# First expert layer: a table of tokens by lane and tile, and rows gathered from a copy in DRAM, in place of per-expert row lists

## The chip, the core and the metric

The kernel runs on one core of a Trainium2 chip. TensorE (PE in the profile) multiplies matrices, VectorE (DVE) and ScalarE (ACT) work on elements, GpSimd (POOL) issues the indirect DMAs and does small elementwise work, and SyncE (SP) issues most of the other DMAs. [...] The metric is the device time of one execution in microseconds (us), as the median of several runs.

## The reference

Four layers follow one another on a batch of 8 x 512 tokens of 256 numbers, each with a residual and a layer norm: a recurrent block of three layers; an expert layer with 8 experts; an attention of 16 heads; a second expert layer with 16 experts, 4 for each token. The change concerns the first expert layer:

```python
logits = xt @ Wg                                   # xt: 4096 x 256
probs = softmax(logits);  pT = probs.T
_, top_idx = top_k(pT, cap)                        # cap = 4096 / 8: each expert picks its tokens
sel = zeros((E, T), bool).at[arange(E)[:, None], top_idx].set(True)
tok2exp = where(sel.any(axis=0), argmax(where(sel, pT, -inf), axis=0), argmax(pT, axis=0))
weights = take_along_axis(probs, tok2exp[:, None], axis=1)[:, 0]
out = sum over e of where(tok2exp == e, weights, 0)[:, None] * (gelu(xt @ W1[e]) @ W2[e])
```

So in the end each token belongs to one expert, and has one weight. The next thing that happens to the result is the layer norm of `x + out`, at the head of the attention layer.

## The kernel before, in words

`x_tok` holds all tokens in SBUF: 128 partitions by 32 chunks (`NC`) of 256 numbers; it is the front part of `x_ext`, whose rows have 276 numbers (`RW`), with room for a gate weight and two row numbers. The stages are these.

1. **Recurrent block** (`recurrent_layers`), 12 pairs of stages. Its SP queue also zeroes the sums of the second expert layer (`acc`) and, at L229, the whole list area `m0rows` in DRAM (8 lists of 4224 rows).
2. **Gates** (`expert_choice_gates`): softmax and a threshold search on DVE and PE; it gives `M`, a one-hot matrix of token and expert, and the weight of each token, written into `x_ext`.
3. **Lists** (`expert_choice_layer` from L1195, class `Lists`). Two products, with ones (`tot`) and with a triangle (`rk`), give each token its place in its expert's list. POOL writes the rows into the lists, one indirect DMA for each of the 32 chunks (`put`, L737); SP closes each list with empty rows (`end_list`, L771). DVE makes two tables: one over the lists' state after half the chunks, from which 8 full tiles (`NE0`) may start early, and one over the rest (`table`, L793 to L826). `fence` (L755) makes POOL wait until the first 16 puts have landed, and then POOL gathers the 8 early tiles (`gather`, L907), with the other puts in between.
4. **Expert tiles** (`Lists.run`): 36 tiles (`ME0`; three more stand in a block that runs only if there are more) of 128 rows of one expert. `turn` transposes the rows (L968, copied at L970), `first` multiplies by W1 and applies gelu (L981, L989), `second` multiplies by W2 (L1003), and `done` adds weight times result to the row (L1261) and scatters the rows to `res` in DRAM (L1264, POOL). The order on PE is first(t), turn(t+1), second(t-1). After second(t-1), tile t+3 is loaded on SP (L960), and its 1 MB of weights if they differ from those of the last tile in the same of four buffers (`NW`; L950, L952). A part of n tiles is dealt out so that each buffer works through n/4 neighbouring entries of the table; the parts are tiles 0 to 7 and 8 to 35. In this stage the order on POOL and SP is the program's.
5. **Rows back** (`rows_back`, L1286): SP loads `res` into `x_tok`, 8 loads of 512 KB, each partition 4 rows of 1 KB that lie one after another. A list row carries the number of the row of `res` that this needs (`place`), so that the tokens come back in another order of the chunks.
6. **Attention** (`attention_layer`), in the program's order on PE, ACT and DVE: layer norm and transposes of each group of four chunks, products for q, k and v, and heads spread over partitions by 8 small DMAs on SP for each half of q or k (`spread_heads`, L1688); the first scores (L1801) need the first half of q's and k's heads. The second expert layer's constants (L728 to L733, L1329 to L1334) are loaded on SP between the rows and the heads.
7. **Second expert layer** (`token_choice_layer`), and the final sums, layer norm and store (L2006 to L2016).

Outside the stages named, a scheduler orders the instructions by program order and readiness.

Of the kernel before, what the change touches and what calls it, by code (L numbers as in the profile page):

```python
# [10 lines left out]
F32 = mybir.dt.float32  # L11
# [6 lines left out]
P = 128  # L18
# [28 lines left out]
NE0 = (NC // 2 * P - E0 * (P - 1)) // P  # L47
# [109 lines left out]
def recurrent_layers(tc, x_tok, xT, lg, ident, eps6, eps5, acc, rows0, a):  # L157
# [11 lines left out]
    with ExitStack() as ctx:  # L169
# [45 lines left out]
        NZ = 1060  # L215
        zero = wp.tile([P, NZ], F32, name="zero1")
        nc.vector.memset(zero, 0.0)
        for x in acc:
            nc.sync.dma_start(
                x[:T, :].rearrange("(p c) d -> p c d", p=P),  # L220
                zero[:, :D].unsqueeze(1).to_broadcast([P, NC, D]),
            )
            nc.sync.dma_start(x[T : T + P, :], zero[:, :D])
# [368 lines left out]
        def late(t):  # L592
# [20 lines left out]
            if N:  # L613
                last_norm(t - 2, 0, NCH)
            inputs(t)
# [22 lines left out]
        def end(u):  # L638
# [20 lines left out]
            last_apply(u - 1, 0, NCH)  # L659
            residual(u, 0)  # L660
# [12 lines left out]
            last_apply(*parts[0])  # L673
            last_apply(*parts[1], on_dve=True)
            for b in (1, 0):
                for i in range(2 * b, 2 * b + 2):
                    last_turn(u, i, on_dve=b == 1)
# [11 lines left out]
class Lists:  # L689
# [6 lines left out]
    def __init__(self, tc, ctx, name, E, NT, a, rows=None):  # L696
# [6 lines left out]
        self.rows = rows  # L703
        if rows is None:
            self.rows = self.dram.tile([E * LT + P, RW], F32, name=f"{name}rows")
# [4 lines left out]
        self.held, self.got = [], {}  # L710
# [171 lines left out]
    def everywhere(self, psum, tag, ident):  # L882


        nc, rp, n = self.nc, self.rp, self.early
        first, spread = rp.tile([P, 1], F32, name="first"), rp.tile([P, n], F32, name="spread")
        nc.vector.tensor_copy(first, self.tabs[0][1][:, 0:1])
        nc.vector.tensor_scalar_mul(spread, ident[:, :n], first)
        self.at_ps = psum.tile([P, n], F32, tag=tag, name="at_ps")
        nc.tensor.matmul(self.at_ps, self.ones, spread, start=True, stop=True)  # L890

    def take_rows(self):
        self.at = self.rp.tile([P, self.early], I32, name="at")
        self.nc.vector.tensor_scalar_add(self.at, self.at_ps, self.pno)

# [7 lines left out]
    def gather(self, t):  # L903

        i = self.entry(t)
        self.got[t] = self.rp.tile([P, RW], F32, name=f"{self.name}got{t}")
        self.reads(self.nc.gpsimd.indirect_dma_start(  # L907
            out=self.got[t], out_offset=None, in_=self.rows[:, :],
            in_offset=bass.IndirectOffsetOnAxis(ap=self.at[:, i : i + 1], axis=0),
            bounds_check=self.E * LT + P - 1, oob_is_err=False,  # L910
        ).ins)
# [11 lines left out]
    def run(self, ctx, ident, w_pack, bias, done, taken=None, besides=None):  # L923
# [16 lines left out]
        xgs, hTs, read = {}, {}, {}  # L940
# [4 lines left out]
        def weights(t):  # L945
            if t < len(self.held):
                return
            w, differs = read.pop(t, None) or known(t)
# [5 lines left out]
        def load(t):  # L954
            if t in self.got:
                xgs[t] = self.got.pop(t)
                return
            xgs[t] = hp.tile([P, RW], F32, tag="xg", bufs=NW + 1, name=f"{nm}xg_{t}")
            at = value(t, 0, E * LT)
            ins = nc.sync.dma_start(xgs[t], self.rows[bass.ds(at, P), :]).ins  # L960
            if t < self.early:
                self.reads(ins)
# [86 lines left out]
        rest(t1)  # L1049

# [125 lines left out]
def expert_choice_layer(tc, pre, x_ext, lg, ident, rows, res, load, a):  # L1176

    nc = tc.nc
    x_tok = x_ext[:, :, :D]
    with ExitStack() as ctx:  # L1180
        L = Lists(tc, ctx, "m0", E0, NT0, a, rows)
        L.constants(a)
# [3 lines left out]
        keep = rp.tile([P, E0, NC], F32, name="keep0")  # L1186
        nc.vector.memset(keep, 1.0)
        nc.vector.memset(keep[:, :, 0:1], 0.0)
        expert_choice_gates(
            nc, rp, psX, ident, lg, a, M, x_ext[:, :, D].rearrange("p (s j) -> p j s", j=2)  # L1190
        )
        load()
# [5 lines left out]
        cnt = rp.tile([P, E0, NC], F32, name="cnt0")  # L1198
        by_expert = tot.rearrange("p c e -> p e c")
        nc.vector.tensor_copy(cnt, by_expert)  # L1200
        nc.vector.tensor_add(cnt[:, :, 0], cnt[:, :, 0], L.off)
        upto = rp.tile([P, E0, NC], F32, name="upto0")
        nc.vector.tensor_tensor_scan(
            upto.rearrange("p e c -> p (e c)"), keep.rearrange("p e c -> p (e c)"),
            cnt.rearrange("p e c -> p (e c)"), 0.0, ALU.mult, ALU.add,
        )
        nc.vector.tensor_sub(cnt, upto, by_expert)
        pl = rp.tile([P, NC, E0], F32, name="pl0")
        slot = rp.tile([P, NC], I32, name="slot0")
        fs = rp.tile([P, NC], F32, name="fs0")  # L1210

        with tc.manual_schedule(engines={mybir.EngineType.DVE, mybir.EngineType.Pool}):
            for i in range(2):
                k = slice(i * NC // 2, (i + 1) * NC // 2)
                nc.vector.tensor_add(pl[:, k], rk[:, k], cnt.rearrange("p e c -> p c e")[:, k])
                nc.vector.tensor_mul(pl[:, k], pl[:, k], M[:, k])
                nc.vector.reduce_sum(fs[:, k], pl[:, k], AX.X)
                nc.vector.tensor_copy(slot[:, k], fs[:, k])
            n, half = (rp.tile([P, E0], F32, name=k) for k in ("n0", "half0"))
            nc.vector.tensor_sub(half, upto[:, :, NC // 2 - 1], L.off)  # L1220
            nc.vector.tensor_sub(n, upto[:, :, NC - 1], L.off)
            L.early, L.breaks = NE0, [ME0]
            L.done = rp.tile([P, E0], F32, name="done0")
            for _, part in L.table(half, 0, 0) + [L.early_tiles()]:
                part()
            L.everywhere(psX, "x", ident)
            for _, part in L.table(n, P - 1, NE0, L.done):
                part()
# [907 lines left out]
```

## Time and profile before

| What | Value |
|---|---|
| Three runs | 1902.87, 1903.4 (median), 1906.02 us |
| Profiled execution, its own time | 1902.39 us |
| Span of its profile | 1900.6 us |
| Granted TensorE clock, mean | 0.946 of full |
| PE, DVE, ACT, POOL busy | 88%, 59%, 52%, 27% of the span |
| Recurrent block ends, gates begin | about 399 us |
| Gates end, lists begin (`tot`) | 453.4 us |
| First transpose of a tile; end of the last product | 488.1; 631.2 us |
| First load of rows back; first scores of the attention | 635.3; 661.6 us |
| Scatters of the second expert layer | 1332 to 1850 us |

The profile is one execution. Times are from the start of its span, which lies 1.8 us inside the execution's own time. PEld is the loading of weights into TensorE, which overlaps the products. A busy time of an engine says little by itself; what counts is which engine the others wait for in each stage. Queues of DMA instructions are SPq, ACTq, POOLq: the time there is that of issuing, not of moving.

### The profile page before, as it was taken

What the parts mean: (1) busy time and instruction counts of PE and PEld (TensorE: products, weight loads), DVE (VectorE), ACT (ScalarE), POOL (GpSimd) and SP (SyncE); (2) the same over time, 40 slices, a digit from 0 to 9 for tenths busy, and PEclk for the clock granted to TensorE, in tenths of its full rate; (3) what the DMA queues carried; (4) which work ended last, traced back from release to release, by engine and by line L of the source; (5) the groups of instructions that cost most, each with busy time, mean ns of one, the idle gap of its engine ahead of it and who ended that gap; (6) DMA issues with size and microseconds to landing.
All of it is one profiled execution on the core that took longest, in us unless ns stands there. A gap on an engine that the chain in (4) does not pass through costs nothing. (4 is left out here: it accounts for less than half of the span.)

```text
span 1900.6 us, 30538 instructions
## 1 busy us (share of the span) xinstructions
PE 1663.6 (88%) x10108; PEld 1086.5 (57%) x10108; DVE 1120.4 (59%) x2827; ACT 992.8 (52%) x2134; POOL 513.2 (27%) x497
## 2 busy tenths in 40 slices
PE   6999997432699799999989999987999999999996
PEld 2555553321699576222222222223889999999985
DVE  6999999775122463777868787884434222222226
ACT  4899986420122342566666766655534333343333
POOL 1000000012622220010221422332666644444440
PEclk9999998765799899999999999998999999999998
DMA  9991000012663400000110111132675658666548
GB/s 357 402 405 42 1 1 0 0 58 101 216 229 122 121 9 6 16 14 18 38 39 18 62 49 30 44 102 75 162 208 129 154 131 230 143 140 140 99 83 266
DMA packets 113249, 211.88 MB, mean 111 GB/s; under 512 B 16749, under 2 KB 84415, under 8 KB 106816
## 3 DMA queue, kind: packets, MB, share of 16 engines
q1 hardware_dynamic: 80672, 161.44, 25.6%
q0 software_dynamic: 29408, 45.80, 11.8%
q10 hardware_dynamic: 3008, 2.63, 0.4%
q8 instruction: 84, 1.38, 0.3%
q14 instruction: 77, 0.63, 0.1%
HBM read 233.05 MB, written 99.12 MB: 175 GB/s over the span
## 5 line engine op out<-in xcount | busy, mean ns | idle before, releaser
L1894 DVE TENSOR_REDUCE nmx<-s 128x1 f32<-128x512 f32 x512 | 329.5, 685 | 125.6 <-PE t L1813 112.4
L1901 ACT ACTIVATE pe<-t 128x512 f32<-128x512 f32 x512 | 277.7, 594 | 184.4 <-PE t L1813 181.4
L1801 PE MATMUL s<-kT,qT 32*128 32x512 f32 x1024 | 289.7, 640 | 46.8 <-ACT pe L1901 27.0
L1813 PE MATMUL t<-qA,kT 32*128 32x512 f32 x1024 | 289.7, 642 | 2.5 <-ACT pe L1901 2.0
L1990 POOL DMA_INDIRECT acc<-y,at x136 | 211.8, 1557 | 244.5 <-DVE at L1983 160.0
L1801 PEld LDWEIGHTS s<-kT,qT 32*128 32x128 f32 x1024 | 78.5, 183 | 195.5 <-ACT pe L1901 182.5
L987 ACT ACTIVATE m1hT<-m1h,m1ws 128x128 f32<-128x128 f32 x272 | 99.4, 367 | 150.5 <-PE m1h L981 135.6
L987 ACT ACTIVATE m1hT<-m1h,xT 128x128 f32<-128x128 f32 x272 | 99.5, 367 | 141.5 <-PE m1h L981 124.5
L1989 DVE TENSOR_SCALAR y<-m1o,gt 128x256 f32<-128x256 f32 x136 | 65.7, 483 | 162.8 <-PE m1o L1003 162.5
L970 DVE COPY m1xq<-m1xp 128x256 f32<-128x256 f32 x136 | 57.6, 423 | 170.7 <-PE m1xp L968 170.5
L737 POOL DMA_INDIRECT m1rows<-x_ext,slot x128 | 127.4, 995 | 113.4 <-ACT pe L1901 73.4
L981 PE MATMUL m1h<-m1xq,xT 128*128 128x128 f32 x1088 | 137.4, 281 | 4.8 <-issue 3.1
L981 PEld LDWEIGHTS m1h<-m1xq,xT 128*128 128x128 f32 x1088 | 135.7, 197 | 8.9 <-issue 3.5
L1837 PE MATMUL po<-pe,V 128*17 128x512 f32 x1024 | 135.6, 602 | 1.2 <-ACT pe L1901 1.2
L981 PEld LDWEIGHTS m1h<-m1xq,m1ws 128*128 128x128 f32 x1088 | 132.7, 193 | 6.9 <-issue 3.6
L981 PE MATMUL m1h<-m1xq,m1ws 128*128 128x128 f32 x1088 | 134.1, 277 | 2.4 <-DVE m1xq L970 2.4
L1003 PE MATMUL m1o<-xT,m1hT 128*128 128x256 f32 x544 | 129.8, 380 | 0.7 <-DVE y L1989 0.5
L1003 PE MATMUL m1o<-m1ws,m1hT 128*128 128x256 f32 x544 | 129.5, 380 | 0.0
L1867 POOL TENSOR_TENSOR AO<-AO,on 128x256 f32<-128x256 f32 x32 | 23.5, 734 | 365.9 <-DVE on L1862 252.3
L1648 POOL MEMSET qT<- 128x512 f32 x2 | 1.0, 524 | 382.2 <-PE lt L522 382.2
L1003 PEld LDWEIGHTS m1o<-xT,m1hT 128*128 128x128 f32 x544 | 97.7, 190 | 11.4 <-issue 1.1
L1003 PEld LDWEIGHTS m1o<-m1ws,m1hT 128*128 128x128 f32 x544 | 98.2, 191 | 10.4
(372 smaller groups left out, 2974.4 us busy)
## 6 DMA issues: line engine op xcount, KB each, us to landing
xT<-in_w_pack SPq DMA_DIRECT2D x68, 1034.0 KB
m1ws<-in_w_pack SPq DMA_DIRECT2D x68, 1034.0 KB
m0ws<-in_w_pack SPq DMA_DIRECT2D x36, 1034.0 KB
m0rows<-zero SPq DMA_DIRECT2D x5, 6360.0 KB
m1xg<-m1rows SPq DMA_DIRECT2D x136, 138.0 KB
acc<-zero SPq DMA_DIRECT2D x2, 4096.0 KB
f<-acc SPq DMA_DIRECT2D x16, 512.0 KB
m0rows<-zero SPq DMA_DIRECT2D x1, 4770.0 KB
```

The lines of the kernel that those rows point to most:

```text
L737: ins = self.nc.gpsimd.indirect_dma_start(out=self.rows[:, :], out_offset=bass.IndirectOffsetOnAxis(ap=place, axis=0), in_=row, in_offset= ...
L970: nc.vector.tensor_copy(xq, ps)
L981: nc.tensor.matmul(ps, w[:, o : o + P], xq[:, dc, :], start=(dc == 0), stop=(dc == DC - 1),)
L987: ins = nc.scalar.activation(hT[:, fc, :], ps, AF.Gelu, bias=w[:, o : o + 1])
L1003: nc.tensor.matmul(ps, hT[:, fc, :], w[:, o : o + D], start=(fc == 0), stop=(fc == FC - 1))
L1801: mm = nc.tensor.matmul(ps, qTs[u % NR][r, qc * P : (qc + 1) * P], kTs[u % NR][r, :], start=True, stop=True,)
L1813: mm = nc.tensor.matmul(ps, kTs[v % NR][r, kc * P : (kc + 1) * P], qAs[v][r, :], start=True, stop=True,)
L1837: mm = nc.tensor.matmul(po[h4 * HP : h4 * HP + VW, :], V[:, b * NQ + kc, 4 * g + h4, :], pes.pop((u, kc, h4)), start=(kc == 0), stop=(kc = ...
L1894: ins = nc.vector.tensor_reduce(at, ps, AX.X, ALU.max, negate=True)
L1901: ins = nc.scalar.activation(pe, ps, AF.Exp)
L1989: nc.vector.tensor_scalar_mul(y, ps, gt)
L1990: nc.gpsimd.indirect_dma_start(out=R.acc[t % 2][:, :], out_offset=bass.IndirectOffsetOnAxis(ap=at, axis=0), in_=y, in_offset=None, compute ...
```

## The change

The lists go. A new class `Gathered` takes the place of `Lists` in the first expert layer (the second keeps `Lists`).

- The recurrent block doesn't zero a list area. When a group of chunks has its last layer norm, SP copies it to `kept` in DRAM (4096 rows of 1 KB, in token order).
- `places` computes for every token its slot in a table of all tiles, each expert's tokens starting on a tile of their own, and splits it into a lane (0 to 127) and a tile. It makes one table of the tiles' experts.
- `invert` turns this round on PE: the sum over the 32 chunks of a one-hot matrix of lanes (128 x 128, made on DVE eight chunks at a time) times a one-hot matrix of 40 tiles that carries the token's number and its weight. The result says for each lane and tile which token stands there (`src`, `dst`) and with which weight (`share`).
- A tile's rows come by an indirect DMA on POOL from `kept` (`fetch`), in the loop and before the loop alike; before, the 28 later tiles came from the lists on SP. The first 36 tiles are one part. Weights are still asked for on SP, the first four after each tile's gather in the program.
- `done` takes weight and destination from the tables; `res` is in token order, so `rows_back` has 32 loads of 128 KB, four for each group, with 32 partitions of four rows of 1 KB each. The third and fourth load of the first group are issued by ACT.

```diff
 def recurrent_layers(...)
-        NZ = 1060
-        zero = wp.tile([P, NZ], F32, name="zero1")
+        zero = wp.tile([P, D], F32, name="zero1")
...
-        n = rows0.shape[0] // P * RW // NZ
-        lists = rows0.rearrange("(p c) w -> p (c w)", p=P).rearrange("p (c z) -> p c z", z=NZ)
-        for c in range(0, n, 12):
-            k = min(n, c + 12) - c
-            nc.sync.dma_start(lists[:, c : c + k], zero.unsqueeze(1).to_broadcast([P, k, NZ]))
...
+        def keep(u, c0, n):
+            l, q = stages[u]
+            at = slice(q * NCH + c0, q * NCH + c0 + n)
+            nc.sync.dma_start(
+                kept.rearrange("(c p) d -> p c d", p=P)[:, at, :], x_tok[:, at, :]
+            )
...
 class Lists:
-    def gather(self, t):
...
+    def fetch(self, t, dst):
+        at = self.value(t, 0, self.E * LT)
+        ins = self.nc.sync.dma_start(dst, self.rows[bass.ds(at, P), :]).ins
...
         def load(t):
-            if t in self.got:
-                xgs[t] = self.got.pop(t)
-                return
...
+            xgs[t] = hp.tile([P, self.width], F32, tag="xg", bufs=NW + 1, name=f"{nm}xg_{t}")
+            self.fetch(t, xgs[t])
...
-        for t in range(0 if bias else NW):
-            weights(t)
-        if besides:
-            besides(-1, None)
-        read.update({t: known(t) for t in range(NW, 0 if bias else self.early)})
         for t in range(NW):
             load(t)
-            if bias:
-                weights(t)
+            weights(t)
...
+class Gathered(Lists):
+    def places(self, M, tot, rk):
+        cnt, upto = (new(k, [P, E, NC]) for k in ("cnt0", "upto0"))
+        by_expert = tot.rearrange("p c e -> p e c")
+        nc.vector.tensor_copy(cnt, by_expert)
+        nc.vector.tensor_tensor_scan(flat(upto), flat(self.keep), flat(cnt), 0.0, ALU.mult, ALU.add)
...
+        nc.vector.tensor_scalar_add(nb_i, upto[:, :, NC - 1], float(P - 1))
+        nc.vector.tensor_single_scalar(nb_i, nb_i, 7, ALU.logical_shift_right)
+        nc.vector.tensor_scalar_mul(nb, nb_i, float(P))
+        nc.vector.tensor_tensor_scan(cum, self.ones[:, :E], nb, 0.0, ALU.mult, ALU.add)
+        nc.vector.tensor_sub(off, cum, nb)
+        nc.vector.tensor_sub(cnt, upto, cnt)
+        nc.vector.tensor_add(cnt, cnt, off.unsqueeze(2).to_broadcast([P, E, NC]))
...
+        nc.vector.tensor_add(pl, rk, cnt.rearrange("p e c -> p c e"))
+        nc.vector.tensor_mul(pl, pl, M)
...
+        nc.vector.reduce_sum(fs, pl, AX.X)
+        nc.vector.tensor_copy(slot, fs)
+        nc.vector.tensor_single_scalar(split[:, 0], slot, P - 1, ALU.bitwise_and)
+        nc.vector.tensor_single_scalar(split[:, 1], slot, 7, ALU.logical_shift_right)
...
+        nc.vector.tensor_copy(self.split, split)
...
+    def invert(self, psum, tag, W):
+        nc, rp, N = self.nc, self.rp, NT0 + 1
...
+        eq, of = new("eq0", [P, NC, N]), new("of0", [P, NC, 2, N])
+        nc.vector.tensor_tensor(eq, row(NC, N), by(self.split[:, 1], NC, N), ALU.is_equal)
+        nc.vector.tensor_mul(of[:, :, 0], eq, by(self.ids, NC, N))
+        nc.vector.tensor_mul(of[:, :, 1], eq, by(W, NC, N))
+        ps = psum.tile([P, 2, N], F32, tag=tag, name="inverse")
+        K = 8
+        for c0 in range(0, NC, K):
+            at = rp.tile([P, K, P], F32, tag="lane", bufs=3, name=f"lane_{c0}")
+            nc.vector.tensor_tensor(
+                at, row(K, P), by(self.split[:, 0, c0 : c0 + K], K, P), ALU.is_equal
+            )
+            for c in range(c0, c0 + K):
+                nc.tensor.matmul(
+                    ps, at[:, c - c0], of[:, c], start=(c == 0), stop=(c == NC - 1)
+                )
...
+        nc.vector.tensor_scalar(self.src, ps[:, 0], -1.0, 0.0, ALU.add, ALU.max)
...
+    def fetch(self, t, dst):
+        i = self.entry(t)
+        self.nc.gpsimd.indirect_dma_start(
+            out=dst, out_offset=None, in_=self.rows[:, :],
+            in_offset=bass.IndirectOffsetOnAxis(ap=self.src[:, i : i + 1], axis=0),
+            bounds_check=T - 1, oob_is_err=False,
+        )
...
 def expert_choice_layer(...)
+        L = Gathered(tc, ctx, "m0", E0, NT0, kept)
+        L.breaks = [ME0]
...
+        with tc.manual_schedule(engines={mybir.EngineType.DVE}):
+            L.places(M, tot, rk)
+            L.invert(psX, "x", W)
...
     def rows_back():
         for g in range(NC // 4):
-            ins = nc.sync.dma_start(
-                x_tok[:, g * 4 : (g + 1) * 4, :], src[:, g * 4 : (g + 1) * 4, :]
-            ).ins
...
+            src = res[g * S : (g + 1) * S, :].rearrange("(i q e) d -> e i q d", q=4, e=4)
+            for e in range(4):
+                queue = nc.scalar if g == 0 and e > 1 else nc.sync
+                ins = queue.dma_start(
+                    x_tok[e * 32 : (e + 1) * 32, g * 4 : (g + 1) * 4, :], src[e]
+                ).ins
```

More of the change, by code (lines that the diff above doesn't have):

```diff
@@ L1207, in expert_choice_layer @@
[L1207 to L1228, printed above, removed]
-            L.ends(n)
-            L.take_rows()
-            L.count_tiles()
-            left = NC
-            def put(k):
-                nonlocal left
-                for c in range(NC - left, NC - left + k):
-                    L.put(slot[:, c : c + 1], x_ext[:, c, :])
-                left -= k
-            put(NC // 2 + 3)
-            L.grown = L.fence(NC // 2)
-            for t in range(NE0):
-                L.gather(t)
-                if t >= NW - 1:
-                    put(min(left, 2))
-            put(left)
@@ L1261, in done @@
             nc.vector.scalar_tensor_tensor(
-                z, ps, row[:, D : D + 1], row[:, :D], ALU.mult, ALU.add
+                z, ps, L.share[:, i : i + 1], row, ALU.mult, ALU.add
             )
@@ L1279, in expert_choice_layer @@
         with tc.manual_schedule(engines={mybir.EngineType.Pool, mybir.EngineType.SP}):
[L1280 to L1281 removed]
+            L.run(ctx, ident, a["w0_pack"], False, done)
     def rows_back():
         for g in range(NC // 4):
[L1286 to L1290 removed]
+            src = res[g * S : (g + 1) * S, :].rearrange("(i q e) d -> e i q d", q=4, e=4)
[4 more added lines that the diff above has]
+                ).ins
+                for last in moved[ME0 - 2 : ME0] + moved[-2:]:
+                    tc.add_manual_dep(ins, last.name, SYNC, reason="all rows are there")
     return rows_back
@@ L2049, in block @@
             weights, load = attention_weights(tc, ep, a)
-            back = expert_choice_layer(tc, pre, x_ext, lg, ident, rows0, res0, load, a)
+            back = expert_choice_layer(tc, pre, x_tok, lg, ident, kept, res0, load, a)
         if stages > 2:
```

151 lines of the change are left out of this document (78 added, 73 removed).

## The prediction, made before the change was run

> **What bounds the kernel now.** I read the page's forty slices first: PE is at 9 or more in most of them and lowest in the eighth to eleventh (4, 3, 2, 6), the end of the recurrent block, the gates and the routing of the first expert layer. The change rewrites the routing and the tiles behind it, so I read those by stage (columns: window; sum; busy time and instructions of PE, PEld, DVE, ACT, POOL; clock; DMA share; GB/s).
>
> ```profile
> 453.00:463.00 10.00, 2.31 (x6) 1.44 (x6) 7.73 (x38) 0.00 (x0) 4.00 (x4) 0.50 0.12 43
> 463.00:473.00 10.00, 0.33 (x2) 0.23 (x2) 2.76 (x23) 1.28 (x1) 7.56 (x9) 0.50 0.94 343
> 473.00:483.00 10.00, 0.00 (x0) 0.00 (x0) 0.00 (x0) 0.00 (x0) 7.08 (x8) 0.50 1.05 380
> 483.00:488.00 5.00, 0.00 (x0) 0.00 (x0) 0.00 (x0) 0.00 (x0) 2.38 (x4) 0.50 0.34 110
> 488.00:498.00 10.00, 9.24 (x46) 8.69 (x47) 1.27 (x3) 2.22 (x8) 7.86 (x8) 0.63 0.34 113
> 560.00:630.00 70.00, 70.00 (x491) 66.16 (x490) 16.82 (x37) 21.07 (x76) 18.46 (x19) 1.00 0.35 112
> ```
>
> From 463 to 488 only POOL works: it writes token rows into the lists. From 488 the tiles keep PE full, to the last product at 631.2. Everything after needs all rows, so a microsecond won before 631 moves the end by one, unless the return of the rows takes it back. The timeline gives the two prices I need most: how a gather becomes a tile, and what a steady tile does.
>
> ```profile
> 484.23 0.10 POOL L755 MEMSET m0full<- 128x1 f32 x1 [2.02 <-DMA m0rows<-x_ext,slot]
> 485.11 1.05 POOL L907 DMA_INDIRECT m0got<-m0rows,at  x1 [0.78 <-POOL m0full L755]
> 488.09 0.66 PE L968 MATMUL m0xp<-ident,m0got 128*128 128x128 f32 x2 [24.77 <-DMA m0got<-m0rows,at]
> ...
> 597.70 1.95 PE L981 MATMUL m0h<-m0xq,m0ws 128*128 128x128 f32 x16
> 597.90 0.48 DVE L1261 SCALAR_TENSOR_TENSOR z<-m0o,m0xg 128x256 f32<-128x256 f32 x1 [1.31 <-PE m0o L1003]
> 598.66 0.97 POOL L1264 DMA_INDIRECT res<-z,m0xg  x1 [2.76 <-DVE z L1261]
> 601.43 1.95 PE L981 MATMUL m0h<-m0xq,m0ws 128*128 128x128 f32 x16
> ```
>
> A gather costs POOL 1.05 us, and PE can use it 1.93 us after POOL is done (486.16 to 488.09). A tile takes 3.73 us (597.70 to 601.43), all of it PE.
>
> **Removed at no gain.** Zeroing the lists moved 36.6 MB (5 x 6360 KB and 4770 KB), with the DMA at share 1.03 from 60 to 120. But the pair of recurrent stages repeats every 25.92 us under that traffic (83.05, 108.97) and without it (160.82, 186.74), and no load waits behind it: 0. What covers it is DVE, busy 29.6 of each 30 us there. The new copy of the rows to DRAM is 4 MB in pieces as each stage ends, on an SP that issues nothing from 123 to 390; the last piece can start at about 395 and is read at 478: 0, and if it blocked SP in front of the threshold search's two constants (issued at 403, used from 405.9) some 2 us.
>
> **The table instead of the lists: -7.5.** Before, the first tile turns at 488.09. After, from the count matrix (DVE free at 454.66 in both): seven instructions over 256 elements at 0.46 to 0.73 start to start (3.65), nine small ones at 0.20 to 0.27 (1.92), the tile table (two reductions 0.53, three small ones 0.35) make 6.45: 461.1, so the weights are asked for at about 462, as now. The one-hot products are 128x1280. A one-hot of the second layer takes 0.424 for 256 elements, an add 1.208 for 1024, so 1.02 ns an element: 1.51 each, three of them, then 1.25 for the first of four lane tiles: 466.9.
>
> ```profile
> L1415 DVE TENSOR_TENSOR hot<-m1iot,fi 128x256 f32<-128x256 f32 x8 | 3.4, 424 | 0.2
> L450 DVE TENSOR_TENSOR x_ext<-x_ext,Y 128x1024 f32<-128x1024 f32 x8 | 9.7, 1208 | 0.0
> ```
>
> PE then runs 32 products, each two passes in this trace, with 128-column weights: 0.198 a pass at clock 0.5 (32 in 6.33 us from 489.89), 0.122 at full clock (16 in 1.95). The clock rose 7.2 us after PE began at 488.09, so 36 passes cold (7.1) and 28 warm (3.4): 477.4; all cold 12.7, all warm 7.8. The DVE's 1.25 for eight products stays ahead. Then a DVE cast 0.2, the wait to POOL 0.3, the gather 1.05, and 1.93: 480.9. The gates begin 0.36 earlier, because two memsets and their kin move behind them: 480.6, a gain of 7.5. Bounds: all warm 10; all cold, with the one-hots 1.5 times slower as the strided 128x256 multiply is (0.653 for 0.425), 3.
>
> **The tile loop: -0.6.** Before it takes 143.1 (488.09 to 631.22). The floor is 1.0 to the first product, 35 x 3.73, and 3.7 for the last tile: 135.3. What is above it is the cold clock at the start and the break after tile 8 (PE idle about 509 and from 519 to 526); the break goes, as 36 tiles become one part. Two costs come.
>
> First the clock: PE rests from 477.4 to 480.9 and hardly works until 482. In this trace the clock fell 4.1 us after the last product (631.2 to 635.3). A cold start costs up to 7.2 x 0.5 = 3.6; I take 2.2, between 0 and 3.6.
>
> Second, each gather now stands on POOL behind the scatter of tile t-1, and is for tile t+3. From the start s of a tile: the sum at s+3.9, scatter s+4.7 to 5.7, gather to s+7.0, usable at s+8.9; PE wants it two tiles on, at s+9.25. So 0.3 us of slack: the period is the larger of 3.73 and (5.2+L)/2, L the time from POOL's end to PE, and L may be 2.25. Quiet gathers have 1.93 (twice: 488.09 and 489.41). The last one before, in a stretch of four weight loads, had 2.99 (505.87 to 508.86). By the reference's routing (201, 475, 844, 242, 658, 908, 367, 401 tokens per expert) seven tiles past the first four load new weights, 1 MB (2.9 us at 365 GB/s) asked for at about s+4.8, beside the gather. Each delays it by between 0 and the 2.2 us that the load still runs: stalls of 0 to 1.9, and 1.06-0.3 by the row above. I take 0.7 each: 5. POOL itself has 2.6 us of work in 3.73. Loop: 142.5.
>
> **The rows' return: +5.5.** Eight loads of 128 partitions x 4 KB become 32 of 32 partitions x 4 x 1 KB; 30 stay on SP, two go to ACT, which is idle. The nearest row is the final store, the same shape in the other direction (ns: least, median, most).
>
> ```profile
> L2016 SPq DMA_DIRECT2D out<-f x32: 569/598/1066, 1869.2 to 1897.1; - x32
> ```
>
> The timeline has today's order on SP, and the instruction that waits for it.
>
> ```profile
> 635.31 6.73 SPq L1286 DMA_DIRECT2D x_ext<-res  x8
> 650.03 5.05 SPq L1688 DMA_DIRECT2D qT<-qks  x8
> 655.17 4.96 SPq L1688 DMA_DIRECT2D kT<-qks  x8
> 661.61 1.13 PE L1801 MATMUL s<-kT,qT 32*128 32x512 f32 x4
> ```
>
> Queued behind the rows on SP are eight constants, then the heads of q and k, which the first scores need. Now SP is done with rows at 642.0, with constants at 649.9 (held by the traffic, share 1.09), and k's first four heads are issued at 657.7; PE takes them at 661.61 without waiting. After: 30 x 0.58 = 17.4, to 652.7; constants 3.4, to 656.1; q 5.1; four heads of k 2.5, to 663.8; landing 2.0 to 2.6 (krow's constant took 2.6 after its issue): 666.1, so +4.5; and 1 to 2 more if the data are slower than the issue. I take +5.5. The first rows come no later (two queues, two loads each). Below: 30 x 0.393, the shortest such load, is hidden in the 649 at which the data end now: +0. Above: 4.2 MB at the 180 GB/s of the final stores (1884 to 1888: 174 and 178, against 399 to 418 for the 128-partition loads at 1866 to 1876) end at 660: +8.
>
> [...]
>
> **Sum.** -7.5 - 0.6 + 5.5 = -2.6. The profiled execution (1902.39, span 1900.6) becomes 1899.8; against the median of the runs, 1903.4, 1.0 higher, it is **1900.8**. A measurement of this kernel can tell 0.2%, 3.8 us, from no change.
>
> **Rivals.** *The return is hidden*: SP issues small loads at 0.393 and data run at full rate; 1895.3, and 1890.3 if the weight loads don't touch the gathers either. For it: 1 KB rows of x came in at 377 GB/s (14 to 24), to all partitions. Against it: the final store. *Slower: the gather bounds the tiles.* From L = 2.25 on every tile pays (L-2.25)/2; at 2.99 that is 0.37 x 34 = 12.6 in place of the 5: 1908.4; with 1.9 at each weight load 1909; both 1917. For it: 0.3 us of slack, and scatters beside weight loads that took 6.8 to land against 2.4. Against it: gathers' median landing is 2.7 from their start, the least. *The change doesn't shorten the stage*: one-hot products and gathers take what the puts took; 1908.3. Against it: the row-by-row sum; for it: a chain of 25 dependent instructions, none of which can be hidden.
>
> **Chances.** Forecast 0.50, own range 1896 to 1906 (of it faster 0.20, same 0.25, slower 0.05); hidden return 0.20, faster; gather-bound 0.22, slower; no shorter 0.08, slower. Faster 0.40, same 0.25, slower 0.35. The range runs from 1891 to 1912; past it lie the rivals' far ends.
>
> **What would show it.** First turn of a tile near 480.6; 64 inverse passes in about 10.5 us; tile period 3.73 with PE waiting for the gather only at the seven loads; last product 8 us earlier than 631.2; SP busy with rows for 17 us; the first scores about 32 us after the rows' first load, not 26.3 (635.31 to 661.61). It would be wrong if PE waits for a gather at every tile, if the first turn is past 484, or if the first scores come within 28 us of that load.

## The result, and the profile after

The changed kernel takes 1933.2 us (median of 4 runs, 1927.4 to 1934.7), the kernel before on the same chip 1903.1: the ratio is 1.015, with a 95% interval of 1.0126 to 1.0174. The prediction was 1900.8, with a range to 1912. The profiled execution has a span of 1932.8 us, 32.2 more than before. A second measurement on another chip gave 1.0129 (1.0109 to 1.0149).

Cut into stages by the timelines, in us (end of one, start of the next; "gates" begin with the first reduction of the logits):

| Stage | Before | After | Difference |
|---|---|---|---|
| Start to gates | 400.6 | 402.8 | +2.2 |
| Gates to first turn of a tile | 87.5 | 82.8 | -4.8 |
| Tile loop, to the end of its last product | 143.1 | 164.3 | +21.2 |
| Last product to first load of rows | 4.1 | 4.0 | -0.1 |
| First load of rows to first scores `s` | 26.3 | 32.5 | +6.2 |
| First `s` to first `t` (L1844, the attention's other product with kT) | 86.8 | 89.9 | +3.1 |
| The rest | 1152.2 | 1156.7 | +4.5 |

So the table does save time, the return costs about what was expected, and the loss is in the loop. The stage windows, read as before (sum; busy time and instructions of PE, PEld, DVE, ACT, POOL; clock; DMA share; GB/s):

```profile
453.00:463.00 10.00, 2.08 (x4) 1.18 (x4) 8.03 (x28) 0.00 (x0) 0.00 (x0) 0.50 0.00 0
463.00:473.00 10.00, 5.08 (x24) 5.11 (x25) 8.24 (x7) 0.00 (x0) 0.00 (x0) 0.50 0.90 352
473.00:483.00 10.00, 8.83 (x42) 8.62 (x41) 0.61 (x4) 0.41 (x1) 0.64 (x1) 0.50 0.17 73
483.00:488.00 5.00, 1.96 (x8) 1.60 (x9) 0.85 (x2) 0.88 (x1) 3.65 (x4) 0.50 0.26 79
560.00:630.00 70.00, 57.86 (x377) 50.91 (x376) 13.11 (x30) 15.54 (x56) 31.20 (x31) 0.98 0.30 102
```

POOL's puts are gone from 463 to 483; DVE and then PE work there instead, PE at clock 0.50. In the last row PE was full before (70.00 of 70); now it works 57.86 and makes 377 passes, not 491. The timeline of PE and POOL in that stretch says what it waits for:

```profile
610.82 1.01 POOL L1295 DMA_INDIRECT res<-z,dst  x1 [1.44 <-DVE z L1292]
...
611.26 0.41 PE L949 MATMUL m0xp<-ident,m0xg 128*128 128x128 f32 x2 [1.25 <-DMA m0xg<-kept,src]
611.51 1.95 PE L962 MATMUL m0h<-m0xq,m0ws 128*128 128x128 f32 x16
...
613.30 1.89 PE L984 MATMUL m0o<-m0ws,m0hT 128*128 128x256 f32 x8
...
615.23 0.48 DVE L1292 SCALAR_TENSOR_TENSOR z<-m0o,share,m0xg 128x256 f32<-128x256 f32 x1 [3.09 <-PE m0o L984]
...
615.99 1.01 POOL L1295 DMA_INDIRECT res<-z,dst  x1 [2.83 <-DVE z L1292]
...
617.31 1.03 POOL L1131 DMA_INDIRECT m0xg<-kept,src  x1 [0.30 <-PE m0h L962]
...
620.23 0.41 PE L949 MATMUL m0xp<-ident,m0xg 128*128 128x128 f32 x2 [1.21 <-DMA m0xg<-kept,src]
```

Read it as a ring. A turn at 611.26 lets the two products behind it run; their sum starts at 615.23, POOL scatters it at 615.99, only then gathers at 617.31, and PE can turn these rows at 620.23, 1.89 after POOL was done. That is 8.97 us for a ring of two tiles, 4.49 a tile where 3.73 was expected, and the gather itself is as quick as any. What is different is where the turn stands. The order of the instructions on PE (T turn, F first, S second, with the tile's number; read off the timelines by counting passes) is this, first in the kernel before, then after:

```
T8 F8 ... T9 S8 F9 T10 S9 F10 T11 S10 F11 T12 S11 F12 T13 S12 F13
after, tiles 4 to 12:    F4 T5 S3 F5 T6 S4 F6 T7 S5 F7 T8 S6 F8 T9 S7
after, from tile 13 on:  T14 S12 F13 (mixed) ... T22 F20 S20 T23 F21 S21 T24 F22 S22
```

The program writes first(t), turn(t+1), second(t-1), but in this stage only POOL and SP follow the program; PE's order is the scheduler's. The description of the kernel before gives the program's order as PE's; its trace has first(t), turn(t+1), second(t) instead. After, tiles 4 to 12 run in the program's order; from tile 13 on the turn comes earlier, mixed with the products at first, and from tile 22 on as turn(t+2) ahead of first(t). Counted from the `second` whose sum the gather has to wait for, the rows are now wanted one `first`, 1.78 us, earlier than I had counted.

The timeline of the return on SP, with the first scores that wait for it (start, us, engine or queue, what it does):

```profile
653.83 20.68 SPq L1317 DMA_DIRECT2D x_ext<-res  x30
679.12 5.01 SPq L1719 DMA_DIRECT2D qT<-qks  x8
684.24 4.95 SPq L1719 DMA_DIRECT2D kT<-qks  x8
686.29 2.58 PE L1832 MATMUL s<-kT,qT 32*128 32x512 f32 x4 [4.68 <-DMA kT<-qks]
```

### The profile page after: what moved, and what is told of

Same layout as the page of the kernel before. It is cut to its first block, busy times and chain, and to the rows that moved or that the text cites. A ratio compares the mean times of both kernels' runs of the same rounds, so it can differ in the third digit from the quotient of the medians.

```text
span 1932.8 us, 30539 instructions
## 1 busy us (share of the span) xinstructions
PE 1692.9 (88%) x10170; PEld 1100.6 (57%) x10170; DVE 1123.5 (58%) x2800; ACT 993.6 (51%) x2134; POOL 509.9 (26%) x487
## 4 chain that ended last, share of the span: by engine, by line
PE 59%; DVE 6%; DMA 4%; ACT 4%; issue 3%; POOL 2%; SPq 1%; POOLq 0%; ACTq 0%; DVEq 0%
PE s L1832 13%; PE m1h L962 12%; PE m1o L984 12%; PE po L1868 6%; PE qk L1703 3%; PE m0h L962 2%; DMA m0xg<-kept,src 2%; PE bv L1794 2%; ACT pe L1932 2%; DVE nmx L1925 2%; PE m0o L984 2%; PE m1xp L949 1%; PE v L1770 1%; PE t L1844 1%; DVE hit L1190 1%
## 5 line engine op out<-in xcount | busy, mean ns | idle before, releaser
L1832 PE MATMUL s<-kT,qT 32*128 32x512 f32 x1024 | 294.2, 648 | 51.4 <-ACT pe L1932 27.0
L1844 PE MATMUL t<-qA,kT 32*128 32x512 f32 x1024 | 292.8, 648 | 2.5 <-ACT pe L1932 2.0
L970 ACT ACTIVATE m0hT<-m0h 128x128 f32<-128x128 f32 x144 | 40.0, 278 | 124.6 <-PE m0h L962 121.1
```

The costliest lines, as they stand in the source:

```text
L1832: mm = nc.tensor.matmul(ps, qTs[u % NR][r, qc * P : (qc + 1) * P], kTs[u % NR][r, :], start=True, stop=True,)
L1844: mm = nc.tensor.matmul(ps, kTs[v % NR][r, kc * P : (kc + 1) * P], qAs[v][r, :], start=True, stop=True,)
```

## The experiments

Stage durations from each profile, in us. A number of this table that is the same work in two kernels can be set side by side; the last column is the ratio to the kernel before on the chip of that run. Those chips differ: the kernel before took 1906 beside e5 to e7 and the repeated changed kernel, 1922 beside e1 to e4 and 1921 beside e8 to e13, and on the last two chips the changed kernel itself was not run. So a ratio is compared only within one of these three groups. It also means different things in them: e11, whose stages sum to those of the changed kernel within 2 us, is 0.6% above the kernel before on its chip, not 1.3 to 1.5. The kernel before loses some 18 us there, and no profile of it on that chip says where.

| Kernel | Gates to first turn | Loop | Rows to first `s` | `s` to `t` | Ratio to before (95%) |
|---|---|---|---|---|---|
| before | 87.5 | 143.1 | 26.3 | 86.8 | 1 |
| after, again | 82.8 | 162.2 | 31.9 | 89.0 | 1.0129 (1.0109 to 1.0149) |
| e1 PE order | 82.8 | 149.1 | 32.4 | 90.7 | 0.998 (0.9967 to 0.9994) |
| e2 gather first | 82.8 | 152.9 | 31.9 | 89.8 | 1.000 (0.9984 to 1.0016) |
| e3 return in 8 | 82.8 | 166.9 | 27.9 | 86.8 | 1.0018 (1.0001 to 1.0035) |
| e4 warm, with a gap | 83.0 | 161.2 | 31.2 | 87.3 | 1.0042 (1.0027 to 1.0058) |
| e5 loop, both | 82.8 | 140.4 | 32.2 | 90.7 | 1.0003 (0.9991 to 1.0016) |
| e6 loop and return | 82.8 | 140.3 | 28.3 | 86.8 | 0.9949 (0.9933 to 0.9965) |
| e7 return in 16 | 82.8 | 165.3 | 101.6 | 90.5 | one run |
| e8 e6, warm | 76.6 | 140.0 | 28.0 | 86.8 | 0.9879 (0.9863 to 0.9896) |
| e9 no loads | 82.8 | 144.3 | 32.1 | 89.1 | one run |
| e10 e8, busy behind the loop | 77.4 | 140.4 | 32.5 | 86.8 | 0.9888 (0.9872 to 0.9905) |
| e11 constants first | 82.8 | 166.0 | 33.1 | 86.8 | one run |
| e12 wide inverse | 80.3 | 163.2 | 31.8 | 90.4 | one run |
| e13 e8, table early | 78.1 | 137.9 | 25.9 | 86.8 | 0.9847 (0.9824 to 0.987) |

**The loop: e1, e2, e5, e9.** My theory after the result was that the moved turn takes 1.8 us from the gather's time. The rival was that the gathers are slow in themselves.

```diff
 e1, around L.run
-        with tc.manual_schedule(engines={mybir.EngineType.Pool, mybir.EngineType.SP}):
+        with tc.manual_schedule(engines={
+            mybir.EngineType.Pool, mybir.EngineType.SP, mybir.EngineType.PE
+        }):
 e2, in steps(); e5 has both edits
                 if t > t0:
-                    second(t - 1)
                     if t + NW - 1 < t1:
                         load(t + NW - 1)
+                    second(t - 1)
+                    if t + NW - 1 < t1:
                         weights(t + NW - 1)
```

> The changed kernel with TensorE's order in the tile loop written out as the program has it: first(t), turn(t+1), second(t-1), in place of the scheduler's, which from tile 13 on puts turn(t+2) ahead of first(t). Nothing else differs. Theory (the moved turn takes 1.8 us from the gather's time): the rows are wanted 1.8 us later, as in tiles 4 to 12 of the changed kernel, whose period was 4.19 (500.03 to 533.56); the loop falls from 164.3 to between 143 (3.73 a tile) and 153 (4.19), the whole by 11 to 21 us, to 1912 to 1922; turns wait for a gather only beside the seven real weight loads. Rival (the gathers are slow in themselves, held up in the DMA by the other transfers, whatever the order on TensorE): the turn waits as much longer as it comes earlier; loop 160 or more, whole within 4 us of 1933.

Loop 149.1: the theory's range holds, the rival's 160 does not. Past the first tile the turns' waits for a gather fall from 19.7 us (19 turns) to 6.5 (8 turns). From the view of waits from 484 to 655 (us in total, times, longest), the first line is the changed kernel's, the second e1's, whose first tile's wait lies ahead of 484:

```profile
PE m0xp L949 <- DMA m0xg<-kept,src: 23.4, 20, 3.7
```

```profile
PE m0xp L949 <- DMA m0xg<-kept,src: 6.5, 8, 2.4
```

> The changed kernel with the gather of tile t+3 ahead of the scatter of tile t-1 on POOL instead of behind it; TensorE's order stays as the scheduler made it, turn two tiles ahead. Theory (the gather is late because it waits for the scatter, which waits for the sum): each gather is issued one tile earlier, 3.7 us, which covers the 1.8 us of the moved turn and a landing of up to 4 us; loop 143 to 146, whole 18 to 21 us less than the changed kernel, 1912 to 1915. Rival (the gathers are slow in themselves): POOL's issue comes earlier, the landing grows by as much, loop 160 or more, whole within 4 us of 1933.

Loop 152.9, between the two. Tiles 4 to 20 ran without a wait for rows, 3.7 us each, their rows lying ready for 2 to 4 us; then the order on PE, made anew by the scheduler, moved the turns on by one more tile (T22 T23 F20 S20 T24 F21 S21), and from tile 23 on every turn but one waited again. So the theory's "order stays" was wrong, and its mechanism fits what came instead: what the gather gained, the scheduler's earlier turn used up. e5, which fixes the order, tests that.

> The changed kernel with both edits of the loop: TensorE in the program's order, and the gather of tile t+3 ahead of the scatter of tile t-1. Theory (the loop is lost to the time between a gather's issue and its turn, which the scheduler's early turns use up again: with the scatter's place alone changed, tiles 4 to 22 ran at 3.73 without a wait, and the turns then moved a third tile ahead): nothing waits for a gather past the first four tiles; loop 142 to 146; 18 to 21 us less than the changed kernel. Rival (behind tile 23 the gathers are slow because of the seven weight loads, not of the order): loop 149 or more, as with one edit alone.

Loop 140.4, better than forecast and 2.7 below the kernel before, whose loop had the break behind tile 8. Of all the turns only the first waits for a gather. The same view of e5 (the changed kernel's line stands above):

```profile
PE m0xp L949 <- DMA m0xg<-kept,src: 3.7, 1, 3.7
```

In time, e5 is 1.2% below the changed kernel on the same chip (1906.2 against 1930.2). The rival, slow gathers, falls: L, the time from POOL's end to PE, was 1.9 in the changed kernel's late tiles (27 to 34).

> TensorE in the program's order, gather behind the scatter, and none of the seven later weight loads: tiles past the first four use the weights that lie in their buffer, so the experts' part is wrong for them. It prices the weight loads in the chain of the gather: with the loads this order took 149.1, with the gather first 140.4. Theory of the prediction (a gather is late only beside a load, L 1.9 to 2.2 else, slack 0.3): loop 140.5 to 143. Rival (scatters and other gathers make a gather late as well; L is over 2.5 at many tiles with no load near): 145 or more.

```diff
 e9 is e1 with, in weights(t):
-            else:
+            elif bias:
                 nc.sync.dma_start(ws[t % NW], w, cond=differs)
```

Loop 144.3, between both. Against e5 (140.4), the program's order with the gather behind the scatter pays 8.7 us in e1: 4.8 for the seven loads, 3.9 without them. The 4.8 are nearly all one wait: tile 24's turn waits 2.4 us in e1 and not at all in e9, and behind it `second` takes 3.30 us, not 1.89, and the next `first` 2.27, not 1.95. These 1.7 us are what 3.4 us at a half clock would cost, an estimate; the changed kernel's clock was at a half that long (from 582.8) behind its own wait of 2.6. In the 3.9 eight turns (tiles 7, 10, 12, 18, 22, 28, 32 and 35) wait 0.2 to 0.9 us for a late gather (L 2.6 to 3.2, where the order leaves room for 2.2); the same eight wait in e1, so e1's theory of waits beside the loads alone is wrong. What made these gathers late isn't shown.

**The return: e3, e7, e11, e13.** e3 makes from each token's number the place that it had in `res` before, and loads the rows as before.

```diff
 e3, in invert(); the four parts are joined by two ORs and copied to 'to'
-        nc.vector.scalar_tensor_tensor(self.dst, none, -1.0, ps[:, 0], ALU.add, ALU.add)
+        for k, (by_, mask, op) in enumerate((
+            (1, 0x3E0, ALU.logical_shift_left), (7, 0x1C, ALU.logical_shift_right),
+            (2, 3, ALU.logical_shift_right),
+        )):
+            nc.vector.tensor_scalar(bits[:, k], self.src, by_, mask, op, ALU.bitwise_and)
+        nc.vector.tensor_scalar(
+            bits[:, 3], self.src, 3, 10, ALU.bitwise_and, ALU.logical_shift_left
+        )
...
+        nc.vector.tensor_add(self.dst, none, to)
 and rows_back() as in the kernel before: 8 loads of 128 partitions x 4 KB
```

> The changed kernel with the rows of the result written to the places that they had before, so that they come back in 8 loads of 128 partitions x 4 KB; the places are made from the token numbers by eight small integer operations on DVE behind the inverse. Theory (SP's 30 issues of 0.64 us hold up the constants and the heads of q and k behind them, and TensorE, idle for it, goes back to half clock): the first scores come 26 to 27 us after the first load of rows, not 32.5, and the 3 us lost just behind them come back: 8 to 9 us less, 1924 to 1925. Rival (the return costs what it did because the attention waits for something else): under 3 us less.

The first scores came 27.9 us after the first load, 1 more than hoped, and the 3.1 us behind them were gone: 7.7 less in these two stages. In the changed kernel PE rests 4.7 us while it waits for the heads, its clock falls to a half, for 6.8 us from 685, and the first four passes of `s` take 2.58 us. In e3 PE goes from the transposes straight to these passes (684.59), and they take 1.13. By my estimate 6.8 us at a half cost up to 3.4, so the rest can account for the 3.1. The number of loads can't: e11 and e4 keep the 32 loads, and `s` to `t` takes 86.8 and 87.3.

> The changed kernel with the 32 loads of the return joined by twos: 16 loads of 64 partitions x 4 rows of 1 KB, one of the first two on ACT. Theory (each issue takes SP 0.6 us, whatever it carries): rows issued in 9 to 11 us, not 20.7; the first scores 27 to 29 us after the first load of rows, not 32.5. Rival (the 1 KB pieces set the rate of about 200 GB/s, or an issue takes twice as long for twice the pieces): the rows still take 18 us or more, first scores 31 us or more after the first load.

```diff
-            for e in range(4):
+            for e in range(0, 4, 2):
...
-                    x_tok[e * 32 : (e + 1) * 32, g * 4 : (g + 1) * 4, :], src[e]
+                    x_tok[e * 32 : (e + 2) * 32, g * 4 : (g + 1) * 4, :], src[e : e + 2]
```

Neither theory foresaw this: 2001 us. From its timeline the loads on SP's queue, and then a stage window with the columns of above:

```profile
653.90 82.02 SPq L1317 DMA_DIRECT2D x_ext<-res  x15
```

```profile
660.00:680.00 20.00, 2.76 (x8) 1.48 (x8) 2.02 (x10) 3.65 (x6) 2.37 (x4) 0.50 0.14 47
```

47 GB/s at a DMA share of 0.14, which is 2.2 of 16 engines; the changed kernel moved 225 GB/s at 1.04 (656 to 660). The slowest dimension of the source's pattern has become 2, where it was 32, and a load now has 64 partitions, not 32; which of the two slows it isn't shown. 15 loads of 256 KB in 82.02 us are 48 GB/s, so SP's issues went at the pace of the data, and this run says nothing on the price of an issue.

> The changed kernel with the eight constants of the second expert layer ahead of the rows on SP instead of behind them. Theory (SP's issue is what the first scores wait for): they come 3.5 to 4.2 us earlier from the first load of rows, 28 to 29 us behind it. Rival (the data of the rows, or ACT's work behind them, set it): still 31.5 to 32.5.

The constants moved ahead of the rows, and the rows behind them: 33.1 from the first load (on ACT): no gain, as the rival has it. But SP began with the constants only at 656.55, because they wait for the end of the tiles as the rows do; from there to the first scores it was 32.6, as from SP's first row load in the changed kernel (32.5). The sum of what SP issues ahead of k's heads decides, in whatever order. The expectation had counted the constants as free.

**The inverse: e4, e8, e12.**

```diff
 e4, ahead of the tables
+        busy = psX.tile([P, 2, 4 * P], F32, tag="s", bufs=1, name="busy")
+        for i in range(22):
+            nc.tensor.matmul(busy[:, 0, : E0 * NC], L.ones, L.keep.rearrange("p e c -> p (e c)"),
+                             start=True, stop=True)
 e8 is e6 with these, and behind 'eq' in invert()
+        for i in range(9):
+            nc.tensor.matmul(busy[:, 0, :256], self.ones, eq.rearrange("p c n -> p (c n)")[:, :256],
+                             start=True, stop=True)
 e12, in the changed kernel
-        nc, rp, N = self.nc, self.rp, NT0 + 1
+        nc, rp, N = self.nc, self.rp, 64
```

> The changed kernel with 22 products of 128x256 without use on TensorE between the count products and the inverse, while DVE makes the tables. Theory (the 64 inverse passes took 13.9 us, 0.217 each, because the granted clock was a half): they run at 0.122 behind the one-hots, 8 us, the first turn comes 5 to 6 us earlier, about 480, and the first tiles save 1.7 us more where the gather lets them; whole 4 to 7 us less, 1926 to 1929. Rival (the products wait for the one-hots or the weight loads, whatever the clock): first turn within 1 us of 485.5, whole the same.

No gain in the stage (83.0): the 22 products ended at 463.6, PE rested 4.3 us, the clock fell at 469 and stayed at a half to the end of the inverse.

> The kernel with all three edits (loop order, gather first, return in 8 loads), and products without use on TensorE from before the count products up to the inverse: 22 as in the run that had them alone, where TensorE then rested 4.3 us and the clock fell again at 469, and 9 more that read the tile one-hot, so that it doesn't rest. Theory (the 13.5 us of the inverse are the half clock): clock 1 until past 478, the inverse takes 8 to 9 us, the first turn comes 5 us earlier from the start of the gates (78 us behind it, not 82.8), and the first tiles, which began at half clock, save 2 more: 5 to 8 us less than the kernel with the three edits alone. Rival (DVE's lane one-hots or the gathers set it): first turn within 1.5 us of 82.8.

Gates to first turn 76.6, a gain of 6.2, a little over the forecast. The clock is 1.00 through the inverse, as e8's window shows (columns as above):

```profile
468.00:475.00 7.00, 7.00 (x63) 7.00 (x64) 3.19 (x3) 0.00 (x0) 0.00 (x0) 1.00 0.96 399
```

It fell at 478, in the wait for the first gather, so the first tiles still ran at a half, and the loop did not change.

> The changed kernel with the inverse's tables 64 tiles wide in place of 40, so that each of its 64 passes has 128 columns, not 80; the 24 further tiles are empty. Theory (narrow passes between weight loads count as too little work, so the clock stays at a half for 13.9 us, though TensorE never rests; the 128-column products of the tiles brought it up 5 us after their start): the clock rises 3 to 7 us after the first pass, and the 64 passes take 9 to 12 us, no longer than the narrow ones. Rival (the clock stays down for another reason): half clock throughout, 64 passes of 0.22 to 0.28, so 14 to 18 us. In both DVE's one-hots take some 2.7 us more.

The clock rose 3.5 us after the first pass (470.6 to 474.1):

```profile
470.00:474.00 4.00, 3.35 (x16) 3.38 (x17) 2.77 (x3) 0.00 (x0) 0.00 (x0) 0.50 1.01 424
474.00:478.00 4.00, 4.00 (x37) 4.00 (x37) 1.23 (x1) 0.00 (x0) 0.00 (x0) 0.99 0.28 112
```

The inverse in the changed kernel, in e12 and in e8 (ns: least, median, most; first and last start):

```profile
L1118 PE MATMUL inverse<-of,lane x64: 421/421/470, 467.9 to 481.4; 128*128 128x80 f32 x64
```

```profile
L1118 PE MATMUL inverse<-of,lane x64: 274/275/551, 470.6 to 479.4; 128*128 128x128 f32 x64
```

```profile
L1124 PE MATMUL inverse<-of,lane x64: 275/275/308, 467.9 to 475.0; 128*128 128x80 f32 x64
```

From the first start to the last, 64 passes of 128 columns take 8.7 us, of 80 columns 13.5: the wider ones are quicker, because they bring the clock up, and the first turn came 2.5 us earlier although the one-hots took 2.4 longer.

**The best of it: e6, e10, e13.**

> Both edits of the loop and the return in 8 loads. Theory (the three costs are apart and add up): 26 to 29 us less than the changed kernel; the first scores 27 to 28 us after the first load of rows; against the kernel before, table -4.8, loop +0 to +3, return +1.5, so within 0.2% of it, on the faster side. Rival (what one saves, the next stage's wait takes back): 22 us less or fewer.

0.9949 of the kernel before, and 1.7% below the changed kernel on the same chip (1897.4 against 1930.2). The savings add up: 32.8 us by these medians, 25.7 by the spans of the two profiles, 26 to 29 expected. Against the kernel before it is better than the 0.2% expected.

> The warmed kernel with two more edits behind the loop: 28 products without use on TensorE behind the last tile, while the rows are scattered and come back, and a square root without use at the head of the attention on ACT, so that its table is loaded before the first statistics come. Theory: the first scores come 26 us, not 28.3, after the first load of rows, and the first transposes and q products run at full clock: 3 to 5 us less than with the warmed inverse alone; 8 to 12 us less than the kernel with three edits; 0.9 to 1.2% less than the kernel before. Rival (the return of the data sets the first scores): under 1 us.

```diff
 e10, in done() behind the last tile's scatter; e13 has only the second edit
+            if t == ME0 - 1:
+                for i in range(28):
+                    nc.tensor.matmul(ps, L.ones, L.keep.rearrange("p e c -> p (e c)"),
+                                     start=True, stop=True)
 at the head of the attention
+            nc.scalar.activation(warmed, eps5, AF.Sqrt)
```

A miss: the first scores came 32.5 us after the first load, and the time is that of e8. The products run from 621.3 to 633.7, ahead of the branch over the unused tiles (L1015). SP asks for the rows at 624.74, but ACT, DVE and POOL go on only when PE reaches that branch, at 633.8 to 633.9, as e10's timeline has it for ACT:

```profile
624.74 6.94 SPq L1347 DMA_DIRECT2D x_ext<-res  x8
633.79 0.20 ACT L1988 ACTIVATE warmed<-eps 128x1 f32<-128x1 f32 x1 [13.65 <-PEq L1015]
```

> The kernel with the three edits and the warmed inverse, and a square root without use at the head of the attention on ACT, so that its table is loaded before the first statistics; nothing is put ahead of the branch. Theory (the table's 1.28 us stands between the first statistics and the first transposes since ACT waits ahead of it): the first scores come 26.3 to 27 us after the first load of rows, not 28.0 to 28.3; 1 to 2 us less than the warmed kernel. Rival (the issues on SP set the first scores, whatever ACT does): 27.8 or more, no gain.

25.9, better than the theory and than the kernel before. In the changed kernel the table load stands behind the first statistics; in e13 it is done before the rows are asked for, as it was in the kernel before (630.76, rows at 635.31). The timelines of ACT, first the changed kernel's, then e13's:

```profile
660.32 1.28 ACT L1734 ACT_TABLE_LOAD   x1 [11.90 <-DVE mv_m L1730]
```

```profile
616.71 1.28 ACT L1982 ACT_TABLE_LOAD   x1 [1.27 <-ACTq L1015]
```

e13 is the fastest kernel here, 0.9847 of the kernel before on its chip. Part of that is not the change: the warm products could stand in front of other stages as well. Part is the chip, on which the kernel before is 1% slower than on the first: by the spans of the profiles e13 is 7.8 us, 0.4%, below the kernel before on the first chip. And part of what it gains on e8 (6.5 us by the medians, 2.0 by the profiles) is luck: its loop is 2.1 us shorter, with the same instructions in the loop.

## Why the prediction was wrong, step by step

- **The failed step: the loop, -0.6, measured +21.2.** "PE wants it two tiles on, at s+9.25. So 0.3 us of slack: the period is the larger of 3.73 and (5.2+L)/2." The 9.25 is two tiles and a `first` in the program's order, first(t), turn(t+1), second(t-1), which I took for PE's order. But PE's order is the scheduler's: it was another in the kernel before (T9 S8 F9 T10 S9), and in the changed kernel the turn moved ahead and took the slack with it. Why the scheduler moved it isn't shown. With the turn one `first` earlier the same formula reads (7.0+L)/2, which for L = 1.9 gives 4.45; measured 4.49. e1 and e5 show it: the written order alone takes 15.2 us out, and with the gather ahead of the scatter all of the loss goes. The cold start was too small as well: with no late gather the loop took 140.0 to 140.4 in e5, e6, e8 and e10 (in e8 the clock came up 9.6 us after the first turn), and 137.9 in e13; the sum had 137.5 (135.3 and 2.2).
- **The rival that came in, for another reason.** "The gather bounds the tiles" had the right end and the wrong switch: it asked for L above 2.25, and L was 1.9 where the ring ran at 4.49 a tile; only single gathers were later, the latest 4.0. I gave its price as 12.6 at L = 2.99; the loop lost 21.
- **The weight loads, 0.7 each, 5 in all.** In the program's order they cost 4.8 (e1 against e9). The sum is right by luck: one load cost 4.1, a wait of 2.4 and 1.7 by which the products behind it took longer, and the others next to nothing. The 3.9 us of late gathers with no load near were not foreseen.
- **The table, -7.5, measured -4.8.** By its terms: DVE's tables 5.9, not 6.45; the one-hots as forecast; gather to turn as forecast. The mis-sized term is the inverse, "36 passes cold (7.1) and 28 warm (3.4)": all 64 were cold, 13.9, and a pass took 0.217, not 0.198. I let the clock rise 7.2 us after PE's start, as it did for the tiles' 128-column products; with 80 columns it didn't rise in 13.9 us while PE worked without a pause (467.9 to 481.8), and with 128 it did, after 3.5 us (e12).
- **The rows' return, +5.5, measured +6.2, and right in its mechanism.** 30 issues of 0.60 with 0.04 between, 20.7 us and not 17.4: I had left out the gap and one issue of 1.71. Not foreseen: 3.1 behind the first scores, where the clock falls after PE's rest (e3). In the kernels with 8 loads, where SP is done earlier, the table load on ACT costs 2.1 more (e13 against e8). The issue, not the data, is the limit: it takes the same 0.60 when the DMA share is 0.62 (668 to 672) and when it is 1.04 (656 to 660).
- **Zeroing and the kept copy, 0.** The gates begin between 399.8 and 403.4 in the kernels that have the change, at 400.6 before; the +2.2 of the profile lies in that spread. Its clock was at a half for two more stretches of 3.4 us than before; that this is the cause isn't shown. Right, within 3 us.
- **The rest, +4.5.** From the first `t` to the start of the attention's last product with V the changed kernel took 569.6 both times, the one before 565.4; the kernels here, all with the same code in that stage, took 563 to 572. The clock was at a half for 17.1 us of that stage in the changed kernel and for 6.8 in the one before, in different places. Not put down to the change; it stays open.

The signs that the prediction named would have shown it at once: first turn past 484 (485.5), and PE waiting for a gather at nearly every second tile.

## What to carry to other kernels

The order that a program writes need not be the order on an engine, and a scheduler may choose another after a change; before a slack is worked out from it, find out which engines follow the program, compare with the trace, and write the order out by hand where a slack of tenths decides. Put a prefetch ahead of the store on the same queue, so that the next tile's rows don't wait for the last tile's result (loop 149.1 in e1, 140.4 in e5). And price a chain of small products at a clock that such products were seen to run at, not at that of the products nearby: the 64 passes here took 13.9 us at a half and 7.3 at full clock (e8).

## What the runs showed of the hardware

- Loads of 64 partitions whose source pattern has 2 as its slowest dimension ran at 47 GB/s (e7), those of 32 partitions with 32 at about 200 (changed kernel, 167 to 225 from 656 to 675).
- Passes of 80 columns between 128x128 weight loads left the clock at a half for 13.9 us, passes of 128 raised it after 3.5 (e12); at full clock, the 80-column passes kept it up (e8).
- In the tile loop a rest of TensorE of 2.6 us (changed kernel) was followed by 3.4 us of half clock, and one of 2.4 (e1) by products that took 1.7 us longer; rests of 2.0 (changed kernel) and 2.2 (e2) were followed by neither.
- With 32 partitions and pieces of 1 KB a load, 225 GB/s moved at a DMA share of 1.04; the 128-partition loads of the kernel before, with 4 KB a partition, moved 349 at 1.03. First the changed kernel's window, then the window of before:

```profile
656.00:660.00 4.00, 0.00 (x0) 0.00 (x0) 1.43 (x6) 0.00 (x0) 4.00 (x9) 0.50 1.04 225
```

```profile
637.00:641.00 4.00, 0.00 (x0) 0.00 (x0) 1.68 (x8) 0.06 (x1) 1.25 (x2) 0.50 1.03 349
```

That is 0.64 of the rate. Partitions and pieces changed together, so which of them sets the rate isn't shown; and SP's issue (128 KB in 0.64 us, 204 GB/s) comes first.
